# Row sum chains in three pairs of entry 0 of a two-layer graph attention kernel, and other buffers for two of its tiles

## The chip, the cores and the metric

The kernel runs on one core of a Trainium2 chip. The metric is device time in microseconds (us) of one execution. Three runs of the kernel before gave 4280.04, 4280.19 and 4282.62 us, median 4280.19. The core has five engines with a queue each: TensorE (PE in the profile, PEld for its weight loads), VectorE (DVE), ScalarE (ACT), GpSimd (POOL) and SyncE (SP), which issues nearly all of the DMAs here. An engine takes its instructions in the order in which they stand in its queue and waits on semaphores for the others.

## The reference

Eight batch entries (2048 nodes with 256 features) pass through two attention layers over one graph `adj`. Only the first layer is touched by the change:

```python
x_proj = jnp.einsum('bnd,hdf->bhnf', x, W)              # 8 heads of 32 features
e_src = jnp.einsum('bhnf,hf->bhn', x_proj, a_src)
e_dst = jnp.einsum('bhnf,hf->bhn', x_proj, a_dst)
e = jax.nn.leaky_relu(e_src[..., :, None] + e_dst[..., None, :], ALPHA)
beta = jax.nn.softplus(beta_tilde)
e = e + (beta * jnp.log(prior + EPS))[:, None, :, :]    # prior is adj
e = jnp.where(adj[None, None, :, :] > 0, e, neg_inf)
attn = jax.nn.softmax(e, axis=-1)
h = jnp.einsum('bhij,bhjf->bhif', attn, x_proj)
...
return h @ W_out.T
```

The sum of this and x goes through a layer norm; then comes a dot product attention layer with `leaky_relu`, the same mask, softmax, `relu` and another layer norm.

The softmax of layer 0 is a row of numerators divided by their sum. The kernel writes the numerators as a product: a factor m for each pair of nodes, which is the same for all heads and entries, times the larger of two terms that need only one number per query and one per key (`s` below), times a factor per key (`re`, second half). So each head needs a weighted sum of value rows (`val`) and the plain sum of its numerators (`den`).

## The kernel before

**Tiles and loops.** Everything is fp32. Keys go in 16 tiles of 128 (`jt`), queries along the free dimension (2048). Heads are taken in four pairs (`hp`), two heads at a time. `Gat` is layer 0 of one entry, `Dot` is layer 1. One unit of work of `Gat.step` is one key tile of one pair: 4 pairs of 16 tiles, 64 units an entry.

**One unit.** For each of the two heads one VectorE instruction makes the 128x2048 tile `s` from `c` (one number per query, the same in all partitions), a column of `re` and the tile `mt` of m^T (line 381, SCALAR_TENSOR_TENSOR, max then mult). TensorE then multiplies `s` by the value rows into `val` and by the key factors, spread over 32 columns, into `den` (`products`, line 414: eight matmuls a call in the code, sixteen records in the trace). At the last tile `finish` copies `val` and `den` out (lines 429 and 431, ACT), sends `den` through DRAM to get the reciprocals 1/den in a compact form (`rc`, lines 435 to 439), and after every second pair loads these back, spread over the partitions, as `rb` (line 451), with which `ht` is multiplied (line 457, DVE).

**Sum chains.** `SUMMED[b][hp]` names key tiles whose `den` matmuls are replaced: the first named tile is scaled by its key factor on ACT into a sum `d` (line 399), each further one is added to `d` by one more VectorE instruction per head (line 394), and one call with a weight of ones brings `d` into `den` at the end of the pair (the call under `if chain and jt == NT - 1`). In the kernel before, entry 0 has no chains; entry 1 has chains of six tiles and the later entries of eight, in their pairs 1 to 3.

**Where m^T comes from.** Pair 0 of entry 0 builds m from `adj` and transposes it (`make_m`, `make_mt`), writes it to DRAM (`mt_d`) and uses it. Every later pair loads it again, 1 MB a tile: `load_mt`, line 208. In pairs 1 to 3 of entry 0 these tiles land by turns in the tag "mt" (two buffers) and the tag "d" (two buffers). The `rb` tiles of entry 0 also use "d". The `s` tiles live in the ring "s" of eight buffers, as do `m` and, from pair 2 on, the second `ht`. `c` has two buffers ("c"): the two loads for the next pair (line 319) each wait for the last `s` instruction that reads the old tile.

**What goes beside entry 0.** After every second unit of entry 0 PE also projects rows of the other seven entries (`others`): loads of `x` (`xg`, line 173, one buffer), transposes (`tr`, line 181), projections (`proj`, line 274), ACT copies (lines 276 and 278), stores to `v_d` (line 657), and once per entry a few small VectorE instructions (`top`, `cs`, `both`, lines 284 to 289).

**What sets the order.** TensorE's order is the order of the code (`manual_schedule`), throughout. SP's is so from entry 1 on; in entry 0 a scheduler places SP's instructions, and it places those of DVE and ACT everywhere. A wait at the head of SP's queue holds back all loads behind it.

Of the kernel before, what the change touches and what calls it, by code (L numbers as in the profile page):

```python
# [27 lines left out]
def kernel(  # L28
# [33 lines left out]
    HALF = N // 2  # L62
    HP = 2
    NP = H // HP
    IG = BK // P


    SUMMED = [[()] * NP, [()] + [(0, 3, 6, 8, 11, 14)] * (NP - 1)]
    SUMMED += [[()] + [tuple(range(0, NT, 2))] * (NP - 1)] * (B - 2)

    const = ctx.enter_context(tc.tile_pool(name="const", bufs=1))
# [11 lines left out]
    def ring_tile(name, shape=(P, N)):  # L83


        return wide.tile(list(shape), F32, tag="s", name=name, bufs=8)

    def wide_tile(name, tag, bufs, dtype=F32):
        return wide.tile([P, N], dtype, tag=tag, name=name, bufs=bufs)
# [114 lines left out]
        return mt  # L204

    def load_mt(jt, tag="mt"):
        mt = wide_tile("mt", tag, 2)
        nc.sync.dma_start(mt, mt_d[ts(jt, P), :])
        return mt

# [29 lines left out]
    class Gat:  # L240
# [81 lines left out]
        def load_ahead(self):  # L322

            self.mt_loads = (load_mt(jt, "d" if hp == 0 and jt in (4, 5, 8, 9) else "mt")
                             for b in range(self.b, B) for hp in range(NP) for jt in range(NT))
            self.c_loads = (gats[b].query_rows(h) for b in range(self.b, B) for h in range(H))
            self.mts, self.cs_ahead = [], []
            for _ in range(HP):  # L330
                self.cs_ahead.append(next(self.c_loads))
                self.mts.append(next(self.mt_loads))
# [13 lines left out]
        def step(self, count=1):  # L346

            for _ in range(count):
                hp, jt = next(self.units)
                for work in list(self.later):  # L350
                    if next(work, self) is self:
                        self.later.remove(work)
                if hp == NP - 1 and jt == 0 and self.b + 1 < B:
                    gats[self.b + 1].load_factors()

                at = self.b * NP + hp + 1
                if at < B * NP:
                    gat = gats[at // NP]
                    if jt == 4 and gat.b > 0:
                        gat.load(at % NP)  # L360
                    elif jt == 12:
                        gat.scale(at % NP)
                if jt == 0:
                    if self.b > 0:
                        self.cs = [self.cs_ahead.pop(0) for _ in range(HP)]
                    else:
                        self.cs = [self.query_rows(hp * HP + a) for a in range(HP)]
                    self.val = pacc.tile([P, HALF], F32, tag="val", name="val")
                    self.den = pacc.tile([P, HALF], F32, tag="den", name="den")
                first = self.b == 0 and hp == 0  # L370
                if first:
                    self.more_mt(jt + 2, jt > 0)
                if self.b > 0:
                    mt = self.mts.pop(0)
                else:
                    mt = self.mts[jt] if first else load_mt(jt, ("mt", "d")[jt % 2])
                s = []
                for a in range(HP):
                    h = hp * HP + a
                    sa = ring_tile("s")  # L380
                    nc.vector.scalar_tensor_tensor(sa, self.cs[a], self.re[:, 0, jt, h:h + 1], mt, ALU.max, ALU.mult)  # L381
                    s.append(sa)
                    if self.b > 0 and jt == NT - 1:
                        self.cs_ahead += [c for c in [next(self.c_loads, None)] if c]
                if self.b > 0:
                    ahead = 2 if hp > 0 or not 1 < jt < 10 else min(4, 11 - jt)
                    while len(self.mts) < ahead and (mt := next(self.mt_loads, None)):
                        self.mts.append(mt)
                v, e = self.v[hp], self.re[:, 1]
                heads = [hp * HP + a for a in range(HP)]  # L390
                chain = SUMMED[self.b][hp]
                if jt - 1 in chain[1:]:
                    for d, sa, h in zip(self.sums, self.last, heads):
                        nc.vector.scalar_tensor_tensor(d, sa, e[:, jt - 1, h:h + 1], d, ALU.mult, ALU.add)  # L394
                self.last = s
                if jt in chain[:1]:
                    self.sums = [wide_tile("d", "d", 2) for _ in heads]
                    for d, sa, h in zip(self.sums, s, heads):
                        nc.scalar.activation(d, sa, AF.Copy, scale=e[:, jt, h:h + 1])
                self.products(self.val, [v[:, jt, ts(a, DH)] for a in range(HP)], s, jt == 0, jt == NT - 1)  # L400
                if jt not in chain:
                    self.products(self.den, [e[:, jt, h:h + 1].to_broadcast([P, DH]) for h in heads], s,
                                  jt == min(set(range(NT)) - set(chain)), not chain and jt == NT - 1)
                if chain and jt == NT - 1:
                    self.products(self.den, [ones] * HP, self.sums, False, True)
                if jt == NT - 1:
                    work = self.finish(hp)
                    next(work)
                    self.later.append(work)
# [8 lines left out]
        def finish(self, hp):  # L418

            b, lo = self.b, hp % 2 * HP * DH
            if hp == 0:
                self.ht = [whole.tile([P, N], F32, tag="heads", name="ht")]
            elif hp == HP:
                self.ht.append(ring_tile("ht"))
            ht = self.ht[hp // HP]
            for s in range(2):
                nc.scalar.copy(ht[lo:lo + HP * DH, ts(s, HALF)], self.val[ts(s, HP * DH), :])
            dn = chunk.tile([P, HALF], F32, tag="ht", name="dn", bufs=4)  # L430
            nc.scalar.copy(dn, self.den)
            yield
            yield
            rc = small.tile([P, HALF // DH], F32, name="rc", bufs=1)
            nc.sync.dma_start(rc, dn[::DH, :].rearrange("q (p c) -> q p c", c=HALF // DH))
            nc.vector.reciprocal(rc, rc)
            yield
            for s in range(2):
                nc.sync.dma_start(rec_d[b, hp // 2, s, hp % 2].rearrange("a (p c) -> (a p) c", c=HALF // DH),
                                  rc[ts(s, HP * DH), :])  # L440
            if lo == 0:
                return
            yield
            rbs = []
            for s in range(2):
                if b == 0:
                    rb = wide_tile("rb", "d", 2)[:, 0:HALF]
                else:
                    rb = chunk.tile([P, HALF], F32, tag="ht", name="rb", bufs=4)
                for a in range(2 * HP):  # L450
                    nc.sync.dma_start(rb[ts(a, DH), :],
                                      rec_d[b, hp // 2, s, a // HP, a % HP:a % HP + 1, :].to_broadcast([DH, HALF]))
                rbs.append(rb)
                yield
            for s, rb in enumerate(rbs):
                half = ht[:, ts(s, HALF)]
                nc.vector.tensor_mul(half, half, rb)
                yield
# [298 lines left out]
```

## Time and profile before

| | us |
|---|---|
| median of three runs | 4280.19 |
| the profiled execution | 4279.62 |
| its span in the trace | 4277.8 |
| PE busy over the span | 4163.8 (97%) |
| DVE busy | 3618.3 (85%) |
| ACT busy | 1609.0 (38%) |

The profiled execution took 1.8 us more than its span, and stands 0.6 us under the median. A busy PE is not one at its peak, since matmuls overlap. Entry 0 takes about the first 11% of the span: pair 0, which builds m^T, ends at about 182 us on DVE, and pairs 1 to 3 at 269, 362 and 455 us (the ends of the last `s` instruction of each, in the timeline of DVE).

In the views, "idle before, releaser" is the time for which an engine had nothing to run ahead of an instruction, and what ended it. L381 is line 381. `a<-b,c` is a tile written and those read; x16 is a count. SPq is the queue of SP, whose time is that of issuing; a DMA's data move after that.

### The profile page before, as it was taken

To read this page: it belongs to the slowest core of one execution; us is meant where nothing else is said; L and a number is where in the kernel's file an instruction comes from. 1 tells how busy PE (TensorE), PEld (TensorE's weight loads), DVE (VectorE), ACT (ScalarE), POOL (GpSimd) and SP (SyncE) were. 2 spreads that over 40 slices of the span, in tenths; PEclk is the share of its full clock that TensorE was granted. 3 is DMA by queue.
4 is the path that set the end of the run, shared out by engine and by line. 5 is a ranking of instruction groups with operands and counts; after the bars stand their busy time and mean duration, and the time that the engine had idled before them with its cause. 6 is when DMAs were issued, how large, how long until landed. Compare 5 with 4: busy or idle time off the path is not lost.

```text
span 4277.8 us, 59110 instructions
## 1 busy us (share of the span) xinstructions
PE 4163.8 (97%) x24928; PEld 2230.3 (52%) x24928; DVE 3618.3 (85%) x2432; ACT 1609.0 (38%) x3007; POOL 10.3 (0%) x14
## 2 busy tenths in 40 slices
PE   7999999999999999999999999999999999999999
PEld 4444355555555555554555555555545555555766
DVE  6888778998899979999799988999799997998222
ACT  6522133333334333342333323333333323343554
POOL 0000000000000000000000000000000000000000
PEclk9999999999999999999999999999999999999999
DMA  7988656657455555555555474556555565553211
GB/s 239 309 287 321 242 210 219 231 203 247 184 201 192 197 205 188 184 196 214 187 208 185 174 248 153 209 187 210 198 191 182 181 233 182 205 182 134 77 49 41
DMA packets 268458, 843.52 MB, mean 197 GB/s; under 512 B 33184, under 2 KB 166304, under 8 KB 194464
## 3 DMA queue, kind: packets, MB, share of 16 engines
q1 hardware_dynamic: 232352, 806.17, 53.2%
q10 hardware_dynamic: 35840, 33.57, 2.3%
q8 instruction: 195, 3.19, 0.3%
q14 instruction: 71, 0.58, 0.0%
HBM read 763.76 MB, written 75.37 MB: 196 GB/s over the span
## 4 chain that ended last, share of the span: by engine, by line
PE 57%; DVE 27%; issue 8%; DMA 5%; ACT 3%; SPq 0%; DVEq 0%; ACTq 0%; POOL 0%; POOLq 0%
DVE s L381 17%; PE acc L596 13%; PE e L554 12%; PE val L414 11%; PE den L414 9%; DVE d L394 6%; PE pt L580 3%; PE h3p L522 2%; DMA mt<-mt_d 2%; PE proj L274 2%; DVE p L559 2%; PE y L483 2%; PE h1p L543 2%; DMA adj_r<-in_adj_dram 1%; DMA adj_t<-in_adj_dram 1%
## 5 line engine op out<-in xcount | busy, mean ns | idle before, releaser
L381 DVE SCALAR_TENSOR_TENSOR s<-c,re,mt 128x2048 f32<-128x2048 f32 x1024 | 2357.5, 2340 | 195.4 <-PE den L414 59.7
L414 PE MATMUL val<-s,v 128*32 128x512 f32 x8192 | 978.8, 597 | 22.0 <-DVE s L381 21.9
L554 PE MATMUL e<-x1t,h 128*128 128x512 f32 x2048 | 964.6, 595 | 21.6 <-ACT pts L582 18.5
L596 PE MATMUL acc<-h,pts 128*128 128x256 f32 x4096 | 905.0, 379 | 0.0
L596 PEld LDWEIGHTS acc<-h,pts 128*128 128x128 f32 x4096 | 777.8, 190 | 156.4 <-issue 57.4
L414 PE MATMUL den<-s,re 128*32 128x512 f32 x5600 | 683.4, 593 | 0.0
L394 DVE SCALAR_TENSOR_TENSOR d<-s,re,d 128x2048 f32<-128x2048 f32 x282 | 654.0, 2343 | 0.0
L414 PEld LDWEIGHTS val<-s,v 128*32 128x32 f32 x8192 | 252.3, 110 | 599.0 <-issue 530.7
L559 DVE CUSTOM_DVE_ANT_0 p<-p,pen 128x2048 f32<-128x2048 f32 x128 | 292.5, 2285 | 260.5 <-ACT p L556 254.4
L554 PEld LDWEIGHTS e<-x1t,h 128*128 128x128 f32 x2048 | 351.2, 190 | 287.6 <-issue 249.8
L556 ACT ACTIVATE p<-e 128x512 f32<-128x512 f32 x512 | 305.2, 596 | 416.9 <-PE e L554 414.3
L562 ACT ACTIVATE p<-p,neg 128x2048 f32<-128x2048 f32 x128 | 256.5, 2004 | 472.2 <-DVE neg L559 472.2
L414 PEld LDWEIGHTS den<-s,re 128*32 128x32 f32 x5600 | 188.9, 110 | 418.8 <-issue 418.8
L580 PEld LDWEIGHTS pt<-ident,p 128*128 128x128 f32 x2048 | 245.2, 141 | 301.5 <-issue 237.5
L582 ACT COPY pts<-pt 128x512 f32<-128x512 f32 x512 | 297.0, 585 | 228.9 <-PE pt L580 226.2
L580 PE MATMUL pt<-ident,p 128*128 128x128 f32 x2048 | 309.8, 276 | 16.0 <-ACT p L562 8.3
L230 ACT ACTIVATE f<-mv,eps_ln 128x1 f32<-128x1 f32 x128 | 37.9, 296 | 434.8 <-DVE mv L228 434.2
L601 ACT ACTIVATE z<-acc,rec 128x256 f32<-128x256 f32 x128 | 60.0, 469 | 250.7 <-PE acc L596 102.4
L274 PE MATMUL proj<-wp,xt 128*128 128x272 f32 (+1 forms) x512 | 130.7, 400 | 4.7 <-ACT xt L182 3.0
L522 PE MATMUL h3p<-w3s,x1t 128*128 128x256 f32 x512 | 122.6, 383 | 6.4 <-ACT x1t L517 4.7
L483 PE MATMUL y<-wot,ht 128*128 128x256 f32 x512 | 119.0, 385 | 3.5 <-ACT x1t L517 2.1
L276 ACT COPY v<-proj 128x256 f32<-128x256 f32 x128 | 47.2, 374 | 197.2 <-PE proj L274 153.7
(88 smaller groups left out, 1895.4 us busy)
## 6 DMA issues: line engine op xcount, KB each, us to landing
mt<-mt_d SPq DMA_DIRECT2D x496, 1024.0 KB
c<-c_d SPq DMA_DIRECT2D x64, 1024.0 KB
pen<-pen_d SPq DMA_DIRECT2D x112, 512.0 KB
xg<-in_x_dram SPq DMA_DIRECT2D x60, 512.0 KB
adj_t<-in_adj_dram SPq DMA_DIRECT2D x16, 1024.0 KB
mt_d<-mt SPq DMA_DIRECT2D x16, 1024.0 KB
rb<-rec_d SPq DMA_DIRECT2D x128, 128.0 KB
x_d<-ht ACTq DMA_DIRECT2D x64, 256.0 KB
```

Of the source, the lines that this page charges most:

```text
L274: nc.tensor.matmul(t[:, 0:cols], xt[kc][:, ts(it % IG, P)], wp[:, kc, 0:cols], start=(kc == 0), stop=(kc == KC - 1))
L381: nc.vector.scalar_tensor_tensor(sa, self.cs[a], self.re[:, 0, jt, h:h + 1], mt, ALU.max, ALU.mult)
L394: nc.vector.scalar_tensor_tensor(d, sa, e[:, jt - 1, h:h + 1], d, ALU.mult, ALU.add)
L414: nc.tensor.matmul(dst[ts(q, DH), ts(c, BK)], weights[q % 2], s[q % 2][:, ds(q // 2 * HALF + c * BK, BK)], start=start, stop=stop)
L522: nc.tensor.matmul(t[:, ts(i, D)], x1t[:, kc, ts(2 * (j - lag) + i, P)], w3s[:, kc, :], start=(kc == 0), stop=(kc == KC - 1))
L554: nc.tensor.matmul(t, self.h1[:, kc, ts(it % IG, P)], self.x1t[:, kc, ts(c, BK)], start=(kc == 0), stop=(kc == KC - 1))
L556: nc.scalar.activation(p[:, ts(c, BK)], t, AF.Prelu, alpha=ALPHA)
L559: nc.vector.tensor_tensor_reduce(p, p, pen, -1.0, FMAX, ALU.add, ALU.min, neg)
L562: nc.scalar.activation(p, p, AF.Exp, bias=neg, scale=-1.0, accum_out=den)
L580: nc.tensor.transpose(t[:, ts(k, P)], p[:, ts(g * IG + k, P)], ident)
L582: nc.scalar.copy(pt, t)
L596: nc.tensor.matmul(acc, pts[g][:, ts(k, P)], self.h3[:, j, :], start=(j == 0), stop=(j == NT - 1))
```

## The change

```diff
-    SUMMED = [[()] * NP, [()] + [(0, 3, 6, 8, 11, 14)] * (NP - 1)]
+    SUMMED = [[()] + [(0, 4, 8, 12)] * (NP - 1), [()] + [(0, 3, 6, 8, 11, 14)] * (NP - 1)]
     SUMMED += [[()] + [tuple(range(0, NT, 2))] * (NP - 1)] * (B - 2)
...
     def load_mt(jt, tag="mt"):
-        mt = wide_tile("mt", tag, 2)
+        mt = wide_tile("mt", tag, 2 if tag != "s" else 8)
         nc.sync.dma_start(mt, mt_d[ts(jt, P), :])
         return mt
...
-                    mt = self.mts[jt] if first else load_mt(jt, ("mt", "d")[jt % 2])
+                    mt = self.mts[jt] if first else load_mt(jt, ("mt", "s")[jt % 2])
...
                 if b == 0:
-                    rb = wide_tile("rb", "d", 2)[:, 0:HALF]
+                    rb = ring_tile("rb")[:, 0:HALF]
```

Pairs 1 to 3 of entry 0 get chains of the tiles 0, 4, 8 and 12. Their sums `d` take the two "d" buffers, which the odd m^T tiles and the `rb` tiles of entry 0 had; those now take buffers of the ring of eight. The order of TensorE changes only by the `den` calls that go and the three that come. The scheduler places the loads, sums and copies of entry 0 anew on SP, DVE and ACT. From the first units of entry 1 on, the instructions of each engine stand in the same order as before.

## Prediction

> **What bounds the kernel now.** The change touches pairs 1 to 3 of entry 0, so I read that stretch. In the timeline of VectorE the last `s` of pairs 0, 1, 2 and 3 ends at 181.9, 269.0, 362.2 and 455.0 us. The busy times of the stretch 182:455 (columns: window, length, then busy us of PE, PEld, DVE, ACT, POOL, granted clock, DMA share, GB/s):
>
> ```profile
> 182.00:455.00 273.00, 268.42 (x2007) 126.82 (x2011) 226.95 (x117) 71.48 (x232) 7.68 (x5) 0.99 0.83 295
> ```
>
> PE is full, but DVE has only 273.0 - 227.0 = 46.0 us left. The waits of DVE in the same window say what that rest is (total us, times, longest):
>
> ```profile
> DVE s L381 <- PE den L414: 12.0, 7, 2.6
> DVE s L381 <- DMA mt<-mt_d: 10.2, 2, 8.9
> DVE top L284 <- ACT both L278: 7.8, 2, 6.7
> DVE s L381 <- PE tr L181: 6.4, 1, 6.4
> DVE ht L457 <- DMA rb<-rec_d: 4.8, 2, 3.8
> DVE cs L287 <- POOL top L285: 1.9, 5, 0.6
> DVE rc L436 <- DMA rc<-dn: 1.8, 1, 1.8
> DVE s L381 <- PE proj L274: 1.0, 1, 1.0
> ```
>
> Only the PE `den` and `proj` rows, 13.0 us, are DVE waiting because PE is behind. The 6.7 and 6.4 stand at the starts of pairs 3 and 2, where `c` is reloaded behind the last `s`. The chain that ended last shows that this matters at the end of entry 0 (start us, us, what):
>
> ```profile
> 442.56 1.72 PE den L414 x16
> ...
> 445.42 4.62 DVE s L381 x2
> 450.06 11.22 DMA c<-c_d
> 461.47 2.36 DVE s L381
> 463.86 2.36 DVE s L381
> 466.24 4.82 DMA mt<-mt_d
> ```
>
> Up to 445 us the chain runs on PE; then it goes through the last `s`, the load of `c` behind it, and entry 1's first tiles. Whatever delays the last `s` delays all that follows.
>
> SP's timeline at the start of pair 1 (start, us, issue) shows its queue waiting for PE:
>
> ```profile
> 188.54 0.38 SPq L173 DMA_DIRECT2D xg<-in_x_dram  x1
> 190.78 0.37 SPq L657 DMA_DIRECT2D v_d<-v  x1
> 191.19 0.69 SPq L435 DMA_DIRECT2D rc<-dn  x1
> 191.99 0.66 SPq L208 DMA_DIRECT2D mt<-mt_d  x1
> 195.68 1.15 SPq L439 DMA_DIRECT2D rec_d<-rc  x2
> ```
>
> `xg` waits for PE's transposes of the `x` rows before it, `v_d` for projections. This is harmless here: the tiles of units 0, 1 and 3 were loaded earlier.
>
> [...] The trace has 2341 ns for L381 and 2343 for L394; back to back 16 of them take 36.28 us (325.91 in the timeline), 2.27 each, which I use. [...] here `mt` took 4.82 and 5.02 us when the engines were free, 8.31 at 182 us when two `c` loads ran beside it. I use 5 to 6, the trace's.
>
> **The change part by part.**
>
> *Removed on PE.* Four `den` calls a pair go and one comes: 3 x 3 = 9 calls of 1.72 us (chain row above), 15.5 us. PE binds in this stretch, so this would be the gain if nothing else took its place.
>
> *Added on DVE.* Three tiles of two heads in three pairs: 18 instructions of L394 x 2.27 = 40.9 us. Of this the 13.0 us of PE waits are cover. The first tile's copy on ACT, 6 x 2.00 us (L399 in entry 1), lies in 71 of 273 us of ACT's load: nothing. The `s` of tile 3, which takes over the buffers of tile 0, now waits for this copy too; it ends before DVE gets there. If ACT were late, DVE would stand 2 us a copy.
>
> *DVE becomes the bound.* A pair is now: wait for `c`, then from the first tile's second head on 31 `s` and 6 `d`, 37 x 2.27 = 84.0; `rc` 0.3; two sets of `top`/`cs`/`both` at 1.3: 86.9 us. Pair 2 has two `ht` products more (2.4), pair 3 one `v` product (1.2). The waits for `c` I keep as they are, from the last `s` to the second head: 6.6, 7.4 and 8.2 us. That is 181.9 + 6.6 + 86.9 + 7.4 + 89.3 + 8.2 + 88.1 = 468.4 against 455.0: **+13.4 us**, with no other stall.
>
> *Moved loads.* This is where I think more is lost. The order of the built program's SP queue puts the loads of odd tiles at a pair's start late, since a ring buffer is free only after PE used it, and behind `xg` loads:
> - Pair 1, tile 1 stands behind the `xg`, `v_d` and `rc` of the fence above, in the place issued at 191.99, and lands at about 198. Tile 0 is there a little earlier (its load is moved ahead of the `c` loads), so DVE is done with it at 190.8 and idles until 198, less 0.3 for `rc`: 6.9. Tile 3 is third in a row of 1 MB loads: 1.
> - Pair 2, tile 1 stands behind an `xg` that waits for the transposes after pair 1's last units: after the last `s`, val, den and the new call (3 x 1.72), four projections (1.84) and eight transposes (1.07) with some lag of PE give 10 us, then 5.5 to land, plus 1 for the 0.5 MB of `xg` ahead. DVE could start it at 7.4 + 2.3 + 0.3 = 10 us: 6.4 lost. Tile 3 stands behind the next `xg`, after tile 1's val and den (3.4), projections and transposes (2.9), four issues (1.5) and the landing (6.3): 14 us after tile 1, where DVE has tile 2 and one `ht` product to do (5.8): 8.2.
> - Pair 3, tile 1 likewise, without PE's lag: 4. Its tile 3 is ahead of the next `xg`: nothing.
> - The other odd tiles are issued 10 us and more before DVE gets to them, by the same count: nothing, but 5 us each if PE falls behind.
> Sum 26.5 us. Each can be zero if PE has the transposes earlier than I count; with landings of 8.3 in place of 5.6 the four big ones cost 11 more, and a cold PE some 4: between 191 and 200 us its granted clock was 0.62, and two units took 9.0 us (195.45 to 204.5) where they take 7.0.
>
> *`rb` and entry 1.* `rb` moved from "d" into the ring no longer waits for two `s`, a step on the old chain (1.4 us of PE wait before `y` at 499.37). But the loads of tiles 4 and 5 of entry 1 now wait for the last `den` call of `d` (PE, about 5 us after the last `s`, before the reciprocals that SP waits for anyway: nothing), and `rb` stands behind three of these loads at the end of the queue, with its product ahead of tile 4 on DVE. I take +1 for both, between -2 and +6.
>
> *Sum.* 13.4 + 26.5 + 1 = +40.9 us, on the profiled execution's 4279.6: 4320.5; the median is 0.6 above it: **4321 us**. After 560 us the order on all engines is that of before and the chain has no slack that I see, so the shift stays.
>
> **Rivals.**
> *DVE's sum alone (A).* SP runs ahead of PE and the new loads land in time: +13 (above) to +28 (40.9 less only the 13.0 of PE waits): 4293 to 4308, middle 4300. For it: the scheduler placed the loads where it thought them early enough. Against: the order of `xg` and `mt` is fixed, and PE waits on DVE.
> *PE's relief wins (B), the faster side.* If DVE's 46.0 us of rest could take the 40.9, PE sets the end: 4279.6 + 0.6 - 15.5 = 4265. It decides from the point where `c`, `mt` and `rb` waits overlap the added work; of 46.0 only 13.0 are PE waits, and the `c` waits come back with every pair. That the change does nothing is no case: 18 L394 and 9 fewer calls stand in the order.
> *More stalls (C).* The ring loses one or two of eight buffers to `mt`, one to `ht` from pair 2 on, so DVE leads PE by some three tiles, not four; with loads tied to PE the later odd tiles stall too, five or so at 5 us: 4345.
>
> **How the numbers follow.** Forecast 0.60 (its own range 4306 to 4336), A 0.22, B 0.05, C 0.13. The range 4296 to 4338 leaves out B, half of C and a quarter of A: 0.17. About 0.2%, 8.6 us, is what a measurement can tell from no change. Slower by more: forecast, C and nearly all of A, 0.92; same 0.03; faster 0.05.
>
> **What would show it.** Right: the last `s` of pairs 1, 2 and 3 at about 283, 395 and 495 us; DVE waits on DMA `mt` of some 25 us between 182 and 495; DVE's waits on PE `den` nearly gone; PE with gaps at the pair starts. A right: the ends at 275 to 290, 372 to 385 and 468 to 483, without those waits. Wrong altogether if PE still shows no gap after 200 us, or if `s` waits on `den` grow.

## Result and profile after

| | before | after |
|---|---|---|
| median, four runs each on one chip (us) | 4280.11 | 4332.66 |
| lowest and highest | 4277.06 to 4282.62 | 4330.19 to 4336.80 |
| the profiled execution, and its span | 4279.62, 4277.8 | 4336.80, 4335.0 |
| last `s` of pairs 0, 1, 2, 3 ends at | 181.9, 269.0, 362.2, 455.0 | 183.7, 291.9, 410.3, 512.7 |

The changed kernel is slower: 52.6 us by the medians, ratio 1.0122, 95% interval 1.0110 to 1.0133. The profiled execution of after is the slowest of its four, 57.2 us over the profiled one of before; of these, 57.7 are there at the last `s` of pair 3, 1.8 of them already at that of pair 0. So nearly all of it happens in pairs 1 to 3 of entry 0, and entry 1 neither adds nor gives back.

The stretch 182:455 of after, in the columns shown before:

```profile
182.00:455.00 273.00, 233.11 (x1518) 103.53 (x1516) 213.48 (x108) 73.20 (x203) 7.32 (x4) 0.93 0.72 250
```

PE was busy for 268.42 us of this stretch, now for 233.11; but DVE, which was to become the bound, is at 213.48, less than before (226.95) although it has more to do. The same stretch holds less of the work in after; over its own three pairs, from 183.7 to 512.7 us, PE is busy for 285.2 and DVE for 268.2 of 329.0 us. No engine is full, and the DMA engines are less busy too (0.72, was 0.83). This is not an engine that became the bound but two engines that wait for each other. What DVE waited for in the same stretch (total us, times, longest):

```profile
DVE s L381 <- DMA mt<-mt_d: 17.1, 7, 5.6
DVE s L381 <- DMA c<-c_d: 16.2, 3, 8.2
DVE ht L457 <- issue: 8.8, 1, 8.8
DVE s L381 <- PE tr L181: 8.2, 1, 8.2
...
DVE s L381 <- PE den L414: 1.3, 1, 1.3
```

The waits for `den` are gone (12.0 before), and loads have taken their place. The wait put down to `tr` is no work of PE's that DVE needs: it ends at 419.28 us, at the start of pair 3, where the `c` loaded behind the last `s` has just landed. The chain of waits shows the path at the start of pair 2, which was not a path before (start us, us, what):

```profile
301.52 0.89 PE tr L181 x8
302.41 0.02 issue
302.43 0.38 SPq L173
302.81 0.05 issue
302.86 7.82 DMA mt<-mt_d
...
313.07 2.36 DVE s L381
315.42 0.04 issue
315.47 2.78 PE val L414 x11
...
323.08 0.89 PE tr L181 x8
323.97 0.02 issue
323.99 0.40 SPq L173
324.39 0.05 issue
324.44 0.49 SPq L451
324.94 0.05 issue
324.99 7.62 DMA mt<-mt_d
```

This is a loop through the queues of PE, SP and DVE and the DMA engines. PE's transposes of `x` rows free the buffer for the next `xg`; SP has stood at that `xg` (L173) and only now comes to the m^T tile behind it; the tile lands 7.8 us later; DVE makes `s` of it; PE, which has run dry, takes `s` and does its projections and transposes, which free the buffer for the next `xg`, behind which the next m^T tile and an `rb` load (L451) stand. Each turn has a landing of 7 to 8 us in it: from 302 to 323 us PE is busy for 14.3 us of 21 and DVE for 12.2. After this gap PE is slow as well: it stood 6.3 us before the `val` at 313.21, and from 313 to 318 us its granted clock is 0.50 and `val` x11 takes 2.78 us; at 503.75 us, after 1.2 us without work, `val` x11 takes 1.49 at a granted clock of 1.00 (503.5 to 506). That the gap is the cause is a reading; no run changes it alone. Over whole pairs, the granted clock in pairs 1, 2 and 3 is 0.94, 0.93 and 0.97, before it was 0.96, 1.00 and 1.00. With the lengths of the pairs this makes an estimate of some 14 us of PE's full speed lost more than before; how much of that lies on the path, no run separates. SP's timeline has the same at the start of pair 1, where tile 1 (193.75) follows the `xg` and `v_d` as forecast:

```profile
190.35 0.38 SPq L173 DMA_DIRECT2D xg<-in_x_dram  x1
192.59 0.37 SPq L657 DMA_DIRECT2D v_d<-v  x1
193.01 0.69 SPq L435 DMA_DIRECT2D rc<-dn  x1
193.75 0.74 SPq L208 DMA_DIRECT2D mt<-mt_d  x1
```

### The profile page after: what moved, and what is told of

The parts are those of the page before. It is cut to its first block, busy times and chain, and to the rows that moved or that the text cites. A ratio compares the mean times of both kernels' runs of the same rounds, so it can differ in the third digit from the quotient of the medians.

```text
span 4335.0 us, 58800 instructions
## 1 busy us (share of the span) xinstructions
PE 4182.3 (96%) x24784; PEld 2231.8 (51%) x24784; DVE 3659.5 (84%) x2450; ACT 1620.5 (37%) x3013; POOL 14.4 (0%) x14
## 4 chain that ended last, share of the span: by engine, by line
PE 52%; DVE 30%; issue 8%; DMA 5%; ACT 3%; SPq 1%; POOL 0%; DVEq 0%; ACTq 0%; POOLq 0%
DVE s L381 19%; PE acc L596 12%; PE e L554 11%; PE val L414 10%; PE den L414 8%; DVE d L394 6%; PE pt L580 3%; DMA mt<-mt_d 3%; PE h3p L522 2%; DVE p L559 2%; PE y L483 2%; PE h1p L543 2%; PE proj L274 1%; DMA adj_t<-in_adj_dram 1%; DMA adj_r<-in_adj_dram 1%
## 5 line engine op out<-in xcount | busy, mean ns | idle before, releaser
L414 PE MATMUL val<-s,v 128*32 128x512 f32 x8192 | 1003.0, 600 | 60.0 <-DVE s L381 59.9
L394 DVE SCALAR_TENSOR_TENSOR d<-s,re,d 128x2048 f32<-128x2048 f32 x300 | 695.7, 2344 | 0.0
L580 PE MATMUL pt<-ident,p 128*128 128x128 f32 x2048 | 309.8, 276 | 15.5 <-ACT p L562 8.3
```

Of the source, the lines that this page charges most:

```text
L414: nc.tensor.matmul(dst[ts(q, DH), ts(c, BK)], weights[q % 2], s[q % 2][:, ds(q // 2 * HALF + c * BK, BK)], start=start, stop=stop)
L580: nc.tensor.transpose(t[:, ts(k, P)], p[:, ts(g * IG + k, P)], ident)
```

## The experiments

Differences are of medians, each against the runs of before on the same chip; intervals are of the ratio (0.1% is 4.3 us). Some expectations take an earlier run's number from its ratio, or from two medians of different chips, and so are up to 1.1 us off the differences given here. Lengths are from the profiled executions, each from the last `s` of a pair to that of the next, in DVE's timeline. In every run the scheduler placed the loads and sums of entry 0 anew, so each edit also brings an order of its own on SP; no run changes the order alone.

| run | pair 1 | pair 2 | pair 3 | median less before | ratio, 95% |
|---|---|---|---|---|---|
| before | 87.1 | 93.2 | 92.8 | | |
| after | 108.2 | 118.4 | 102.4 | +52.6 | 1.0110 to 1.0133 |
| new buffers alone | 102.1 | 112.5 | 101.0 | +40.7 | 1.0078 to 1.0109 |
| chains alone | 99.0 | 99.2 | 93.5 | +14.3 | 1.0020 to 1.0045 |
| after without the adds | 101.6 | 110.4 | 100.9 | +33.9 | 1.0067 to 1.0092 |
| after, ACT issues | 102.0 | 103.0 | 100.6 | +31.1 | 1.0064 to 1.0089 |
| before, ACT issues | 84.5 | 95.4 | 96.3 | +5.5 | 1.0007 to 1.0021 |
| new buffers, ACT issues | 96.4 | 99.4 | 94.9 | +18.2 | 1.0028 to 1.0053 |
| odd m^T tiles in the ring alone | 105.6 | 100.9 | 101.7 | +31.0 | 1.0058 to 1.0085 |
| chains of two, alone | 88.3 | 97.5 | 89.7 | -4.2 | 0.9982 to 0.9999 |
| after, odd loads earlier | 103.5 | 110.0 | 96.3 | +33.1 | 1.0063 to 1.0088 |
| new buffers, ACT, some `s` in "d" | 91.9 | 91.5 | 111.3 | +52.9 | 1.0104 to 1.0132 |
| before, `c` ahead | 83.0 | 102.3 | 92.8 | +6.7 | 1.0009 to 1.0022 |
| `c` ahead, chains for one head | 89.8 | 100.7 | 87.2 | +1.2 | 0.9997 to 1.0014 |

### The two halves of the change

**The new buffers alone.** The chains of entry 0 taken back out of after:

```diff
-    SUMMED = [[()] + [(0, 4, 8, 12)] * (NP - 1), [()] + [(0, 3, 6, 8, 11, 14)] * (NP - 1)]
+    SUMMED = [[()] * NP, [()] + [(0, 3, 6, 8, 11, 14)] * (NP - 1)]
```

> The new places of the odd m^T tiles and of the reciprocals in the ring alone, no row sum chains in entry 0: PE keeps its 9 den calls and DVE has none of the 18 added L394. Theory (DVE's sum costs some 13 us, the late loads at the pair starts the rest): the first odd tiles still come late behind the xg and v_d loads, but DVE has 13.0 us of PE waits as cover and PE stays the bound, so +5 to +20 us, middle +12, with DVE waits on DMA mt of 10 us and more between 182 and 460 us. Rival 1 (the adds on DVE are exposed in full, the moves are harmless): within 3 us of before. Rival 2 (the moves cost what after lost beyond DVE's sum, whatever DVE's load): +30 to +40.

Measured: +40.7 us. The theory's size falls and the second rival's stands, just above its range: the moves cost this much with nothing added on DVE, and although DVE had its 13.0 us of PE waits. DVE's waits from 182 to 500 us:

```profile
DVE s L381 <- DMA mt<-mt_d: 35.5, 16, 4.5
DVE s L381 <- DMA c<-c_d: 16.4, 4, 7.9
...
DVE ht L457 <- DMA rb<-rec_d: 9.1, 1, 9.1
```

The 9.1 us is one `rb`: three of the four small loads for it are out at 302 us, then SP stands at an `xg`, and the last follows it (SP's timeline):

```profile
301.66 0.30 SPq L451 DMA_DIRECT2D rb<-rec_d  x1
312.97 0.40 SPq L173 DMA_DIRECT2D xg<-in_x_dram  x1
313.42 1.38 SPq L451 DMA_DIRECT2D rb<-rec_d  x1
```

That the 13.0 us were no cover fits with when they come. In the trace of before they lie later in the pairs, where DVE leads PE by its `s` buffers: the first of them begin some 66, 40 and 55 us after the last `s` of the pair before. At a pair's start DVE has just spent its lead on the wait for `c`, so a tile that is late there can stop PE too, as at 193.19 us of before, where DVE has waited 8.9 us for tile 0 and PE then 2.8 for its `s`. PE, which was full (268.42 of 273 us), cannot get that back: its own waits for `s` from 182 to 500 us are 24.8 us here, 6.3 before. SP's waits in the same stretch show where the loads are held: 59.9 us at `xg` for PE's transposes and 84.9 at `v_d` for ACT's copies, before 43.0 and 63.8.

**The chains alone.** From before, with the sums in space that entry 0 doesn't use until its second layer:

```diff
+    SUMMED = [[()] + [(0, 4, 8, 12)] * (NP - 1), ...
...
-                    self.sums = [wide_tile("d", "d", 2) for _ in heads]
+                    if self.b == 0:
+                        both_d = whole.tile([P, HP, N], F32, tag="h3", name="d")
+                        self.sums = [both_d[:, a, :] for a in range(HP)]
+                    else:
+                        self.sums = [wide_tile("d", "d", 2) for _ in heads]
```

> The chains of tiles 0, 4, 8 and 12 alone: the sums d lie in space that entry 0 does not use until its second layer, so the odd m^T tiles and the reciprocals stay where they were before. Theory: only DVE's sum is left, +13 to +25 us (4293 to 4305), the last s of pairs 1, 2 and 3 at about 274, 371 and 468 us or some us later by longer waits for c, and no DVE wait on DMA mt over 3 us in pairs 1 to 3. Rival 1 (the adds are exposed in full): +40 to +55, as after. Rival 2 (PE's relief wins once no load is late): -5 to -16.

Measured: +14.3 us, in the theory's range; both rivals fall. Its "no DVE wait on DMA mt over 3 us" is missed, as the 10.2 us below show. The stretch 182:474 (pair 3's last `s` ends at 473.8) shows a DVE that is nearly full:

```profile
182.00:474.00 292.00, 270.73 (x1909) 130.66 (x1913) 266.83 (x136) 85.74 (x248) 11.59 (x5) 0.99 0.79 279
```

Of DVE's 25.2 us of rest, 10.2 are tile 0 of pair 1, whose load stands behind two `c` loads (8.9 before, at the same place), and 9.9 are waits of 5.5 and 4.5 us for `c` at the next two pairs (the view puts the first down to `den`, but it ends as `c` lands). The ends of the pairs are 281.1, 380.3 and 473.8, expected were 274, 371 and 468: the forecast let pair 1 start as after does, with tile 0 loaded ahead of `c`; this kernel doesn't do that, and its second head comes 12.5 us after the last `s` in place of 6.6.

The two halves add up: 14.3 + 40.7 = 55.0, after has 52.6.

**After without the adds** on DVE in entry 0:

```diff
-                if jt - 1 in chain[1:]:
+                if jt - 1 in chain[1:] and self.b > 0:
```

> After, with the 18 multiply-adds of L394 in entry 0 left out, so that the row sums of entry 0 lack the tiles 4, 8 and 12; the copy of tile 0, the 9 fewer den calls and the moved loads stay. Theory: DVE has its 46 us of rest again, PE 15.5 us less, and what is left over is the late loads: between -10 and +15 us against before, middle +5, with DVE waits on DMA mt of some 15 us still there. Rival 1 (the adds are the whole loss): -12 to -16. Rival 2 (the moved loads are the whole loss): +30 and more.

Measured: +33.9 us. The theory (-10 to +15) is missed, and the number is the second rival's; but the moved loads are not the whole loss, since 40.9 us of DVE work less gains 18.7 us on after. 15.5 us of PE work less gains about 7 us on the new buffers alone (40.7). So with the loads as they are, less than half of what either engine has less to do comes off the time.

### Is it the queue?

**After, with ACT as the issuer** of the loads and stores that wait for PE or for copies of its results, so that SP keeps m^T, `c`, `rc` and `rb` (four lines, this is the first):

```diff
-        nc.sync.dma_start(xg, x[b].rearrange("(t p) d -> p t d", p=P)[:, ts(g, IG), :])
+        nc.scalar.dma_start(xg, x[b].rearrange("(t p) d -> p t d", p=P)[:, ts(g, IG), :])
```

The others are those of `v_d` (line 657), `re_d` (660) and `c_d` (306).

> After, with the loads of x (xg), the stores of v and re and the store of the exponentials for c issued by ACT in place of SP, so that an m^T load waits on SP only for its own buffer and for other m^T, c and reciprocal loads. Theory (the loads are late because they stand behind xg and v_d, which wait for PE): most of the mt and rb waits go, +15 to +30 us against before, some 25 less than after. Rival 1 (the ring is short of buffers, the loads wait for their own buffer): +45 to +55, as after, DVE waits on DMA mt unchanged. Rival 2 (ACT stands for PE at each issue and its copies come late): +45 or more with new waits of DVE or PE on ACT.

Measured: +31.1 us, 21.5 less than after, 1.1 above the upper edge of the theory; the rivals' 45 and more fall. DVE's waits for m^T between 182 and 560 us go from 18.7 to 9.1 us.

**Control: before with ACT as the issuer** (the same four lines).

> Control: before with the loads of x, the stores of v and re and the store of the exponentials for c issued by ACT. PE bounds before's stretch and its m^T loads were ahead of the xg and v_d they stand among, so theory: within 5 us of before, -5 to +3. Rival (the queue's waits cost before as well): -8 and more. Rival (ACT's issues delay its copies): +5 and more. What this run gains or loses is to be taken off the gain of after with ACT as the issuer (20.4 us).

Measured: +5.5 us. The theory's interval (-5 to +3) is missed and the number is the last rival's: ACT as the issuer costs something by itself (DVE's waits for `den` are 17.9 us from 182 to 560 us, 12.5 before); that it is by late copies isn't shown. So the queue's order may be worth more in after than the 21.5 us that came back; up to 27 if the control's cost is in both.

**The new buffers alone, with ACT as the issuer.**

> The new places of the odd m^T tiles and of the reciprocals alone, no chains in entry 0, and the same loads and stores issued by ACT. Alone, the new places cost 40.7 us. Theory (the loads stand on SP behind instructions that wait for PE): most of it goes, +5 to +15 us remain. Rival (the ring of eight has too few buffers for s and m^T, whatever the queue): +30 to +40 remain, with DVE waits on DMA mt or on PE den and val. Half and half gives about +20.

Measured: +18.2 us: 22.5 of 40.7 us go. It is the half and half case: theory and rival each hold for a part. SP's waits from 182 to 500 us show what holds the m^T loads (L208) now:

```profile
SPq L208 <- DVE s L381: 146.2, 24, 11.7
SPq L208 <- PE den L414: 46.1, 14, 7.8
```

The first row stands in before too, with 79.2 us, where DVE waits 13.4 us for m^T in all: a load waits until DVE is done with the buffer's old tile. The second isn't in before. It is the ring: an odd tile's buffer held an `s` before, and PE gives it back, not DVE. With SP as the issuer this row is 8.1 us; there the loads stand behind `xg` and `v_d` mostly longer than their buffers take to come free. Together with the chains' 14.3 these 18.2 us make 32.5, and after with ACT as the issuer has 31.1.

With ACT as the issuer SP's 144.8 us of waits at `xg` and `v_d` are gone from its queue; the longest single ones were 10.9 and 13.7 us, where issuing an `xg` takes SP 0.38 us and a `v_d` 0.37 (at 187.75 and 189.99 us). From 182 to 455 us the traffic is 286 GB/s, with SP as the issuer 265, and PE's granted clock 0.99, with SP 0.96. So part of the 22.5 us can be PE's higher clock.

**Odd m^T tiles in the ring, `rb` left in "d"**, without chains (from the new buffers alone):

```diff
-                    rb = ring_tile("rb")[:, 0:HALF]
+                    rb = wide_tile("rb", "d", 2)[:, 0:HALF]
```

> The odd m^T tiles in the ring, but the reciprocals rb where they were before (the two buffers d, which entry 0 now uses for nothing else), no chains in entry 0. Theory: the reciprocals' two waits of DVE (18.3 us in the run with both moves) go or shrink, and the odd tiles keep most of the cost: +22 to +38 us, middle +30. Rival (the reciprocals in the ring do it, as they hold a ring buffer for long): +0 to +12.

Measured: +31.0 us, the theory's middle. Pair 2, where a product with `rb` stands ahead of tile 3, is 100.9 us in place of 112.5, and DVE has no wait for `rb`: the last `rb` load (304.33 us) and the m^T load beside it (303.87) stand ahead of the `xg` of 315.06 us in this order. Pairs 1 and 3 are 3.5 and 0.7 us longer. The intervals of this run and of the new buffers alone overlap, and each pair length is from one execution, so that the 9.7 us between the two runs are not firm.

**After, with the odd loads emitted with the even ones:**

```diff
-                    mt = self.mts[jt] if first else load_mt(jt, ("mt", "s")[jt % 2])
+                    if not first and jt % 2 == 0:
+                        self.mt_even, self.mt_odd = load_mt(jt), load_mt(jt + 1, "s")
+                    mt = self.mts[jt] if first else (self.mt_even, self.mt_odd)[jt % 2]
```

> After, with the load of each odd m^T tile of pairs 1 to 3 emitted with that of the even tile before it, so that it takes its ring buffer two allocations earlier and stands ahead of the xg load at the starts of pairs 2 and 3 (at the start of pair 1 it still stands behind an xg and a v store). Theory (place in SP's queue): the stalls of tile 1 in pairs 2 and 3 go, 10 to 20 us better than after: +32 to +43 us against before. Rival (too few ring buffers): the earlier allocation only moves the shortage to s, +48 to +60.

Measured: +33.1 us, 19.5 less than after. This is in the theory's range. The same work in buffers of the same ring, taken earlier and at another place in the queue, is worth over a third of the loss. It isn't all: at the start of pair 2 the load of tile 1 stands ahead of the `xg`, but the last `rb` load and four m^T loads still follow the `xg` of 319.18 us, and DVE waits 8.4 us for an m^T tile, until 328.36.

### What the ring costs without the queue

**The new buffers, ACT as the issuer, and the `s` of tiles 2, 6, 10 and 14 in the two buffers "d"**, which takes 8 in place of 10 buffers out of the ring for every four tiles:

```diff
-                    sa = ring_tile("s")
+                    sa = ring_tile("s") if self.b > 0 or jt % 4 != 2 else wide_tile("s", "d", 2)
```

> The run with the new places of the odd tiles and of the reciprocals, no chains, and ACT as the issuer (17.6 us over before), with the s of every fourth tile (2, 6, 10, 14) in the two buffers d that entry 0 no longer uses, so that the ring of eight has to give ten buffers for every four tiles no more, but eight. Theory (what ACT as the issuer leaves is the ring's shortage): +4 to +10 us, near the control with ACT as the issuer alone (5.9). Rival (what it leaves is still the loads' place in the queue, or ACT's own delay): +15 to +20.

Measured: +52.9 us. Neither theory nor rival holds. As a test of the ring it was badly made: the edit also holds in pair 0, where the two buffers "d" aren't free. The tiles of `adj` land there (`make_m`), DVE waits 18.8 us for them between 120 and 217 us (before none between 120 and 182), and the pair ended at 216.9 us, 35 us late. Against the run without the edit, pairs 1 and 2 are 4.5 and 7.9 us shorter, as a shortage of ring buffers would have it, and pair 3 is 16.4 us longer, with waits of 6.9 and 7.2 us for m^T. So it settles nothing: what the 18.2 us are made of, between PE's late release of the ring's buffers and ACT as the issuer (5.5 us in the control), stays open.

### Is there a better kernel?

**Chains of two tiles, alone:** as the chains alone, with `(0, 8)`.

> Chains of two tiles (0 and 8) in pairs 1 to 3 of entry 0, sums in space that entry 0 does not use otherwise, all else as before: 6 added L394, 13.6 us on DVE, and 3 den calls fewer, 5.2 us on PE. Theory (DVE has 13.0 us of PE waits as cover, and each us beyond counts): 13.6 against 13.0, and PE 5.2 us less: -4 to +4, middle 0. Rival 1 (added DVE work counts in proportion, as the chains of four with 14.3 us for 18): +4 to +6. Rival 2 (PE's relief wins while DVE's work fits the cover): -4 to -6.

Measured: -4.2 us (4276.56 against 4280.80), ratio 0.9990, interval 0.9982 to 0.9999. This is in the second rival's range and at the theory's edge. It fits the rival's reason, that PE's 5.2 us come through as long as the added DVE work (13.6 us) fits into the PE waits (13.0); one run this near the noise doesn't show it. It is the one kernel here below before, by 0.1%, which is as little as the measurement can tell. Its profiled execution is the slowest of its 13, so that the pair lengths in the table are long for it.

**Before, with `c` loaded ahead.** The first head's `c` of the next pair goes into a spare buffer at tile 6, the second head's into the buffer that the current pair's first head leaves at its last tile; entry 1's first `c` likewise behind the last `s` of the first head.

```diff
+                if self.b == 0 and jt == 6 and hp + 1 < NP:
+                    self.cs_next = [self.query_ahead(hp + 1, 0)]
...
+                    if self.b == 0 and jt == NT - 1 and a == 0:
+                        if hp + 1 < NP:
+                            self.cs_next.append(self.query_ahead(hp + 1, 1))
...
```

> Before, with c loaded ahead in entry 0: one spare buffer of 8 KB a partition (space that entry 0 does not use until its second layer) takes the first head's c of the next pair while the current pair still runs, and the second head's c goes into the buffer that the current pair's first head leaves; no chains in entry 0, the m^T tiles and reciprocals as before. Theory (the waits for c at the pair starts and the 11.2 us in front of entry 1 stop DVE, but PE was full and has only 4.6 us of rest from 182 to 455 us and 11 us from 455 to 560 us): -5 to -14 us, and DVE's waits go over to PE den and val. Rival 1 (the waits for c were hidden by what PE had queued): -3 to +3. Rival 2 (a load of c ahead delays m^T loads): +5 and more.

Measured: +6.7 us. The theory falls, and the number is the second rival's. Pair 1 is 4.1 us shorter, as it should be, and pair 2 is 9.1 us longer. DVE's timeline there:

```profile
307.87 2.36 DVE L480 TENSOR_TENSOR ht<-ht,rb 128x1024 f32<-128x1024 f32 x2 [10.76 <-ACT both L278]
316.08 2.35 DVE L398 SCALAR_TENSOR_TENSOR s<-c,re,mt 128x2048 f32<-128x2048 f32 x1 [5.85 <-DMA mt<-mt_d]
```

The product with `rb` (L457 in before) waits 10.8 us, put down to `both`, which it doesn't read, and the next tile 5.9. On SP the last four `rb` loads are issued from 299.27 us on, 2.1 and 1.7 us behind an m^T tile (297.14) and an `xg` (297.59), and the first product starts 8.6 us after that; the loads of m^T at 309.12 wait on SP for the product, since its `rb` has a buffer of theirs. SP's waits at an `xg` for PE are 1.2 us in all between 296 and 312. So what holds this pair is the late landing of `rb`, and not a long wait at an `xg`. The scheduler gave SP another order in this pair; that a load of `c` ahead delays the others, as the rival has it, isn't separated from that. What loading ahead would bring with the order kept wasn't tried.

**The same with a chain of tiles 0, 4, 8 and 12 for the first head alone**, its sum in the second spare buffer.

> The kernel with c loaded ahead, and a chain of tiles 0, 4, 8 and 12 for the first head of each pair alone (its sum in the other spare buffer of 8 KB): 9 added L394 on DVE, 20.4 us, and 4 half den calls fewer and 1 more in each pair, 9 x 0.86 = 7.7 us off PE. Theory (DVE has the waits for c, some 22 us, and 13.0 us of PE waits as cover): a few us better than c ahead alone, -8 to -18 us against before. Rival 1 (DVE becomes the bound again): no better than c ahead alone, or +3 to +10 us against that run.

Measured: +1.2 us, interval 0.9997 to 1.0014: no difference from before can be told. Against `c` ahead alone its median is 5.4 us lower, so the rival doesn't hold, though the two intervals overlap; the theory's -8 to -18 isn't reached: pair 2 is 100.7 us long, with a wait of 6.3 us for `rb`.

## Why the prediction came out as it did

The direction was right, and so was the mechanism of the larger part, the loads that come late at the starts of the pairs. The forecast was 4321; measured is 4332.66, inside the range, 11.7 us above the forecast, and nearly half way to the rival with more stalls (4345). The other part, DVE as the bound, isn't what after shows. By the runs, the 52.6 us are 14.3 for the chains, some 22 for the order of SP's queue (21.5 and 22.5 come back with ACT as the issuer), and the rest, some 16, is open.

- *Removed on PE, 15.5 us, and nothing gained:* right as to the time. But PE's busy time did not fall: over the three pairs it is 285.2 us, before 268.5 (181.9 to 455), at a granted clock of 0.94 and 0.99 (these stretches end with DVE's `s`, so PE's work in them is not quite the same). The forecast put PE's lower clock at some 4 us and left it out of the sum; the estimate above has some 14. PE's own saving is visible at most where no load is late (chains of two, -4.2).
- *DVE's sum, +13.4:* right by the run of the chains alone, +14.3, but in part by luck. One of its terms was borrowed from after (tile 0 ahead of `c`), and the two differ there by 5.9 us. The last `s` of pair 3 is 18.8 us later than before (473.8, 455.0); then entry 1's second head starts 5.5 us after it in place of 8.9, which gives 3.4 back. As a picture of after it was wrong: DVE is not full there (213.48 of 273 us).
- *The moved loads, 26.5:* the mechanism and the places were right, the sum was low. The run of the new buffers alone has 40.7, and after less the chains' 14.3 has 38.3. Counted by DVE's waits in the profile of after: pair 1, tile 1 forecast 6.9, measured 3.6; pair 2, tile 1 forecast 6.4, measured 5.6; pair 2, tile 3 forecast 8.2, measured 11.6 (8.8 at the `rb` product ahead of it and 2.8 at the tile); pair 3, tile 1 forecast 4, measured 2.7. Together 23.5 where 25.5 were forecast.
- *The step that was mis-sized: "The waits for `c` I keep as they are", 6.6, 7.4 and 8.2 us from the last `s` to the second head.* That is a misreading of before, where these lengths are 11.1, 10.4 and 10.4 us. For pair 2 its timeline of DVE, with the last `s` at 269.0, has

```profile
276.83 2.35 DVE L381 SCALAR_TENSOR_TENSOR s<-c,re,mt 128x2048 f32<-128x2048 f32 x1 [6.44 <-PE tr L181]
279.35 11.40 DVE L381 SCALAR_TENSOR_TENSOR s<-c,re,mt 128x2048 f32<-128x2048 f32 x5 [0.18 <-DMA c<-c_d]
```

  The 7.4 and 8.2 are near the lengths to the first head, 7.8 and 8.2, and leave out that head's own `s`; 6.6 has tile 0 of pair 1 ahead of `c`, which came true, but then `c` itself kept the first head until 191.18. In after the lengths are 9.9, 10.7 and 11.9. So in sum they did stay as they were (32.5, before 31.9), and the sum started 9.7 us too low (22.2). In the chains alone pairs 2 and 3 have 7.9 and 7.3, a gain that the new buffers take away: at the start of pair 3 of after the first `c` load is issued at 408.02 us, behind an `xg`, an m^T tile and a `v_d` of the 2.7 us before it, and its tile is taken 11.3 us later; in the chains alone (379.07) 5.7 us later.
- *Waits for `both`, put at nothing:* DVE's `top` waits for ACT's `both` for 6.9 us between 182 and 495, 7.8 before; the sum has no term for it.
- *"The other odd tiles ...: nothing, but 5 us each if PE falls behind":* three of them came late, by 0.5, 1.3 (pair 1) and 0.7 us (pair 2). With 1.7 for `den` and `proj`, 6.9 for `both` and the 10.3 by which the waits for `c` exceed 22.2, less the 3.0 that the named stalls came out lower (23.5 of 26.5, with the 1 for tile 3 of pair 1), these terms make 18.3. Pairs 1 to 3 of the profiled execution are 16.0 us longer than forecast (329.0, where 86.9 + 89.3 + 88.1 and the waits for `c` and stalls gave 313.0); the 2.3 us over are not accounted for.
- *`rb`, part of "+1":* wrong in place. I counted its loads for entry 1 and gave pair 2 nothing; the run with `rb` left in "d" has pair 2 11.6 us shorter than the new buffers alone, where an `rb` load stands behind the same `xg` as tile 3, and its product stands ahead of tile 3 on DVE. In after part of this lies in the 11.6 us of tile 3 above. In entry 1 `rb` does cost 7.0 us of waiting (546.97 us), but the shift at the end is no larger than at pair 3's last `s`.
- *What would show it:* the last `s` of pairs 1, 2 and 3 was forecast at 283, 395 and 495 us and is at 291.9, 410.3 and 512.7. DVE's waits on m^T were forecast at some 25 us between 182 and 495; they are 17.1, and 25.9 with the `rb` product's wait for the same queue. Waits on `den` nearly gone: yes, 1.3. Gaps of PE at the pair starts: yes.
- *The rivals:* A (DVE's sum alone) falls in after, and is what the chains alone cost. B (PE's relief) is seen at most with chains of two. C hardly holds: later odd tiles stall three times for 2.4 us in all, where it had five or so at 5 us, and the time is nearly half way to its number for other reasons.

Not settled: how the 18.2 us that the new buffers cost with ACT as the issuer divide between the ring's late release and ACT's issues, and what PE's lower clock adds in each run.

## What to carry to other kernels

When a tile moves to another buffer, ask who gives that buffer back and what stands ahead of its load in the issuing queue; a load that waited for the engine that reads it, and now waits for one further down, can close a loop in which both engines idle (from 302 to 323 us above, with PE busy for 14.3 and DVE for 12.2 of 21 us). Read a length that a sum uses between its own two ends: the first and the second head start 2.3 to 2.5 us apart at each of the three pairs of before, and the three lengths were 9.7 us too short in all. Cover counts only where it lies: waits of the second engine late in a stage don't hide a load that is late at the stage's start (13.0 us of such waits in before, and the new buffers alone cost 40.7). And a change of buffers moves the scheduler's whole queue order, so measure the buffer half of a change by itself before the arithmetic half is judged.

## What was not expected of the hardware

The cost of the two halves is additive within the measurement (14.3 + 40.7 against 52.6), although one half makes DVE nearly full (266.83 of 292 us) and the other leaves no engine full (PE 247.17 and DVE 195.31 of 273 us); it is so with ACT as the issuer too (14.3 + 18.2 against 31.1). And the issuer matters without any change in what is moved: 22.5 us for the DMAs of four lines issued by ACT in place of SP, while the same edit costs 5.5 us in the kernel before.
